# Layer 1 of a four-layer kernel: squared halves added before the length matmul, reciprocal lengths spread through DRAM, first image one chunk ahead

## The chip, the cores and the metric

The kernel runs on one core of a Trainium2 chip, in float32 throughout. The metric is the device time of one execution in microseconds (us). Beside the timed runs there is one execution recorded by the hardware profiler; all times inside the kernel come from that one.

## What is computed

The input is four images of 56 x 56 tokens with 256 channels. Four attention-like layers follow one another, each normalised in front and added to its input. The change lies in the second of them (layer 1), whose reference, per image with n = 3136 tokens, is

```python
xn = x / jnp.maximum(jnp.linalg.norm(x, axis=-1, keepdims=True), EPS)
A = jnp.einsum('bnc,cc,bmc->bnm', xn, W_adj, xn)
A = jnp.exp(5.0 * (A - jnp.max(A, axis=-1, keepdims=True)))
A = A * (1.0 - jnp.eye(n, dtype=A.dtype))
A = A / jnp.maximum(jnp.sum(jnp.abs(A), axis=-1, keepdims=True), EPS)
rowsum = jnp.sum(A, axis=-1, keepdims=True)
xW = jnp.einsum('bnc,dc->bnd', x, W_aff)
Ax = jnp.einsum('bnm,bmc->bnc', A, x)
AxW = jnp.einsum('bnc,dc->bnd', Ax, W_aff)
diff = rowsum * (xW + b_aff) - AxW
```

followed by a normalisation over the channels and a leaky ReLU. `x` is here the group-normalised input of the layer. What matters for the change is the first line: every token's vector is scaled to length 1, so each token needs the sum of its 256 squares, and its reciprocal square root has to reach every channel.

## The kernel before

**Layout.** Channels lie on the 128 partitions, in two halves (`CC` = 2); tokens run along the free axis. An image's 3136 tokens are 24 tiles of 128 and a rest of 64 (stored twice, to fill a 25th tile). `tokens` (L1339) prepares an image in seven chunks of up to four tiles: chunks 0 to 5 hold four tiles (512 tokens), chunk 6 (`NC4`) only the rest. Since the channels are on partitions, a sum of squares is a sum over partitions, which TensorE (PE) takes.

**One chunk's steps.** `load` fetches x from DRAM into `x0` (L1349, L1352). `normal(h)` normalises half h on VectorE (DVE, L939) into `xn`; after the second half ScalarE (ACT) squares both into `x0` (L1358). `lengths` sums the squares with matmuls of one column, two per tile (L1366), into PSUM; DVE clips them into `rn` (L1368, one number per token, tokens on partitions), GpSimd (POOL) takes the power -1/2 (L1369) and multiplies it into an identity matrix, `dg` (L1370). `values(i0)` multiplies two tiles by W_aff (L1379) and copies them to `xw` (L953 on DVE or L955 on ACT). `unit_length` multiplies a matrix of ones by `dg` (L1387), which puts every token's reciprocal length on all partitions in PSUM, and DVE multiplies `xn` by it into `xnT` (L1389). For chunk 6, POOL then scales `xdr` (L1393).

**The main work.** A unit is one row tile j and up to four column tiles. `scaled` (L1404, POOL) prepares the row tile `xd`, `logits` (L1411) multiplies it with `xnT`, ACT takes the exponential (L1414), POOL masks the diagonal (L1416), `transposed` transposes the result (L1502, copied at L1505), and `products` multiplies it with `xw` by columns (L1521, added into `acc` by DVE, L1443) and by rows (L1516). A, being symmetric before its rows are divided, is computed once for both. The rest tile has its own forms (`rest_logits` L1453, `rest_products` L1482 and L1486). When a row tile is done, `finish` normalises it on DVE and POOL (L1557 to L1580), and `add` transposes it back (L1587) and adds it to the residual (L1595), which is stored (L1599) while the next one is loaded (L1544).

**What sets the order.** In layer 1 the orders of PE and DVE are those in which the program writes the instructions; those of ACT, POOL and of the DMA queue on SyncE (SP) are set by a scheduler when the kernel is built. Each engine runs its instructions in order. The loop over units calls `small_step` twice per unit; it takes the first entry of the list `small` whose due time has come. The chunks of image b+1 are prepared beside the units of image b: `replace` (L1659), called at row tiles 3, 6, 10, 14, 16, 19 and 23 for chunks 6, 0, 1, 2, 3, 4 and 5, first runs whatever is still pending of earlier chunks (`now`, L1652), loads the chunk, and puts its steps into `small`, due twelve tiles later. `begin` (L1668) runs the pending steps of a chunk at once where a unit needs it. The first image has nothing beside which it could be prepared; a loop of its own (L1628 to L1632) goes through its chunks in order: normalise the next chunk, then `values`, `lengths`, `values` and `unit_length` of this one.

**Buffers.** In layer 1 the PSUM tag "m" has one bank, shared by `lengths`, `values`, `unit_length` and `add`; "v", which the column products use, has two. `x` and `xn` have two buffers each, `dg` one. In the first image the four tags "v", "o", "t" and "s" are used in turn.

Of the kernel before, what the change touches and what calls it, by code (L numbers as in the profile page):

```python
# [24 lines left out]
FP = mybir.dt.float32  # L25
I32 = mybir.dt.int32
AF = mybir.ActivationFunctionType
ALU = mybir.AluOpType
# [3 lines left out]
NIMG = 4  # L32
# [3 lines left out]
P = 128  # L36
CC = C // P
# [14 lines left out]
TINY = 1e-12  # L52
# [778 lines left out]
def direct_blocks(ctx: ExitStack, tc: tile.TileContext, d: dict, watch):  # L831
# [3 lines left out]
    nc = tc.nc  # L835
    const = ctx.enter_context(tc.tile_pool(name="dconst", bufs=1))
    dram = ctx.enter_context(tc.tile_pool(name="ddram", bufs=1, space=bass.MemoryType.DRAM))
    ps = None
    no_step = lambda: None
# [6 lines left out]
    def tokens_of(l, b, t0, n):  # L846
        return stream_of[l][b].rearrange("(h p) t -> p h t", p=P)[:, :, t0:t0 + n]
# [8 lines left out]
    ident = const.tile([P, P], FP, name="ident")  # L856
    make_identity(nc, ident)
    ones = const.tile([P, P], FP, name="ones")
    nc.vector.memset(ones, 1.0)
    mhalf = const.tile([P, CC], FP, name="mhalf")  # L860
# [9 lines left out]
    def psum_tile(tag, bufs, banks=1):  # L870
        shape = [P, 512] if banks == 1 else [P, banks, 512]
        return ps.tile(shape, FP, tag=tag, name="ps_" + tag, bufs=bufs)
# [60 lines left out]
    def known(l, b):  # L933
        while (l, b) not in stats:
            pending.pop(0)()
        return stats[l, b]

    def normalise(dst, src, gst, h):
        nc.vector.tensor_scalar(dst, src, gst[:, h, 0:1], gst[:, h, 1:2], ALU.subtract, ALU.mult)  # L939
# [10 lines left out]
    def evac(i, dst, src):  # L950

        if i % 2:
            nc.vector.tensor_copy(dst, src)  # L953
        else:
            nc.scalar.copy(dst, src)  # L955
# [366 lines left out]
    def layer1(early, big, pool, late, next_layer):  # L1322


        NB, REST = divmod(T, P)
        NC4 = NB // 4
# [5 lines left out]
        xnT = big.tile([P, CC, (NB + 1) * P], FP, name="xnT")  # L1332
        xw = big.tile([P, NB + 1, C + 1], FP, name="xw")
        xdr = big.tile([P, CC, P], FP, name="xdr")
        offd = big.tile([P, P], FP, name="offd")
        nc.vector.tensor_scalar(offd, ident, -1.0, 1.0, ALU.mult, ALU.add)
        nc.vector.memset(xw[:, :, C:], -1.0)

        def tokens(b, c, ps_a=ps_m):  # L1339

            tiles = range(4 * c, min(4 * c + 4, NB + 1))
            k, m = P, len(tiles)
            n = m * P
            box = {}

            def load():
                x = box["x0"] = early.tile([P, CC, 512], FP, tag="x", name="x1")
                if c < NC4:
                    nc.sync.dma_start(out=x[:, :, :n], in_=tokens_of(1, b, 4 * c * P, n))  # L1349
                else:  # L1350
                    for i in range(2):
                        nc.sync.dma_start(out=x[:, :, i * REST:(i + 1) * REST], in_=tokens_of(1, b, NB * P, REST))  # L1352
                box["x"] = early.tile([P, CC, 512], FP, tag="xn", name="xn1")

            def normal(h):
                normalise(box["x"][:, h, :n], box["x0"][:, h, :n], known(1, b), h)
                if h:
                    nc.scalar.activation(box["x0"][:, :, :n], box["x"][:, :, :n], AF.Square)  # L1358

            def lengths():  # L1360
                pm, sq = ps_a(), box["x0"]
                rn = early.tile([P, 4, 1], FP, tag="rn", name="rn")
                dg = box["dg"] = early.tile([P, 4, P], FP, tag="dg", name="dg", bufs=1)
                for i, t in enumerate(tiles):
                    for h in range(CC):
                        nc.tensor.matmul(pm[:k, i:i + 1], lhsT=sq[:, h, i * P:i * P + k], rhs=ones[:, 0:1],  # L1366
                                         start=(h == 0), stop=(h == CC - 1))
                nc.vector.tensor_scalar_max(rn[:k, :m, 0], pm[:k, :m], TINY * TINY)  # L1368
                nc.gpsimd.tensor_tensor(rn[:k, :m, 0], rn[:k, :m, 0], mhalf[:k, 0:1].to_broadcast([k, m]), ALU.pow)  # L1369
                nc.gpsimd.tensor_tensor(  # L1370
                    dg[:k, :m, :k], ident[:k, :k].rearrange("p (o q) -> p o q", o=1).to_broadcast([k, m, k]),
                    rn[:k, :m, :].to_broadcast([k, m, k]), ALU.mult)

            def values(i0):
                pm = ps_a()
                mm = min(2, m - i0)
                for i in range(i0, i0 + mm):
                    for h in range(CC):
                        nc.tensor.matmul(pm[:k, (i - i0) * C:(i - i0 + 1) * C], lhsT=box["x"][:, h, i * P:i * P + k],  # L1379
                                         rhs=w_aff[:, h, :], start=(h == 0), stop=(h == CC - 1))  # L1380
                evac(i0 // 2, xw[:k, 4 * c + i0:4 * c + i0 + mm, :C],
                     pm[:k, :mm * C].rearrange("p (a b) -> p a b", b=C))

            def unit_length():

                pm = ps_a()
                nc.tensor.matmul(pm[:, :n].rearrange("p (m k) -> p m k", k=k), lhsT=ones[:k, :], rhs=box["dg"][:k, :m, :k],  # L1387
                                 start=True, stop=True)
                nc.vector.tensor_tensor(xnT[:, :, 4 * c * P:4 * c * P + n], box["x"][:, :, :n],  # L1389
                                        pm[:, :n].rearrange("p (o k) -> p o k", o=1).to_broadcast([P, CC, n]), ALU.mult)  # L1390
                if c == NC4:
                    for h in range(CC):
                        nc.gpsimd.tensor_scalar_mul(xdr[:, h, :], xnT[:, h, NB * P:], adj[:, h:h + 1])  # L1393

            return [load], [lambda h=h: normal(h) for h in range(CC)], [lambda: values(0), lengths] + [lambda i=i: values(i) for i in range(2, m, 2)] + [unit_length]

        xd, out, xr = {}, {}, {}
        y_rest = late.tile([REST, C + 1], FP, name="yr", bufs=1)
# [214 lines left out]
        for b in range(NIMG):  # L1613
            if b == 0:
                units += [(b, None, q) for q in range(2)]
            for j in range(NB):
# [3 lines left out]
                if b + 1 < NIMG and 0 <= j - 20 < 2:  # L1620
                    units.append((b + 1, None, j - 20))
        turn = iter(range(6 * (NC4 + 1)))
        fresh = [tokens(0, c, lambda: psum_tile(*(("v", 2), ("o", 2), ("t", 1), ("s", 2))[next(turn) % 4])) for c in range(NC4 + 1)]
        for c in range(2):
            fresh[c][0].pop()()
        for step in fresh[0][1]:
            step()
        for c in range(NC4 + 1):  # L1628
            for step in (fresh[c + 1][1] if c < NC4 else []) + fresh[c][2]:
                step()  # L1630
            if c + 2 <= NC4:
                fresh[c + 2][0].pop()()  # L1632
        small, done = [], 0
# [34 lines left out]
        def begin(w):  # L1668
            if w[1] is None:
                for c in (NC4, 2 * w[2], 2 * w[2] + 1):  # L1670
                    now((w[0], c))
                return rest_logits(w[2])
            now((w[0], (w[3] - 1) // 4))
            return logits(*w)
# [3 lines left out]
        for k, w in enumerate(units):  # L1678
            b, j, first = w[:3]
# [11 lines left out]
            ahead = begin(units[k + 1]) if k + 1 < len(units) else None  # L1691
# [567 lines left out]
```

## Time and profile before

| | us |
|---|---|
| median of the three timed runs | 3945.29 |
| their lowest and highest | 3945.14, 3947.95 |
| the profiled execution's own time | 3952.89 |
| its span, first to last instruction | 3951.1 |
| busy: PE, its weight loads (PEld) | 3774.7, 2533.5 |
| busy: DVE, ACT, POOL | 2369.0, 1379.9, 1752.2 |
| layer 1's first image prepared, about | 795 to 848 |
| layer 1's units, about | 848 to 2760 |

In a line of the timeline the columns are the start, the duration, the engine, the source line, the operation, output and inputs, and the shapes; "x8" means that eight instructions follow one another and were merged, and the brackets hold the idle time in front and what ended it. A matmul in float32 is two records. The end of a matmul is modelled, so prices of PE are read from starts. PE, PEld, DVE, ACT and POOL are the engines; SPq is the queue of SP, which issues the DMAs. Clocks are given as a share of full speed.

### The profile page before, as it was taken

How to read it: one execution, taken by the hardware profiler on the slowest of the kernel's cores; microseconds unless marked ns; L12 is line 12 of the kernel's file. 1: busy time of each engine (PE TensorE's matmuls, PEld its weight loads, DVE VectorE, ACT ScalarE, POOL GpSimd, SP SyncE). 2: the span in 40 equal slices, each digit the busy share in tenths (PEclk: the TensorE clock that was granted, in tenths of full speed). 3: DMA queues.
4: the chain of work that ended last, by engine and by line, in shares of the span. 5: the costliest groups of instructions: out<-in, count | busy, mean ns of one | idle time of the engine just before them, and what ended most of it. 6: DMA issues, size and time to landing. Idle time of an engine off the chain costs nothing. (4 is left out here: it accounts for less than half of the span.)

```text
span 3951.1 us, 112757 instructions
## 1 busy us (share of the span) xinstructions
PE 3774.7 (96%) x49095; PEld 2533.5 (64%) x49095; DVE 2369.0 (60%) x4431; ACT 1379.9 (35%) x2927; POOL 1752.2 (44%) x1883
## 2 busy tenths in 40 slices
PE   6899999889999999999999999999999999899998
PEld 3455555557777677776777767776566666455554
DVE  6777777734345544445444553446788888577775
ACT  3354545422222222222222222222555555344443
POOL 2576767721123312233112331124677777555555
PEclk9899999989999999999999999999999999899998
DMA  7343333320000100001000000001344443434443
GB/s 266 101 140 118 120 116 113 101 105 1 25 19 25 40 3 18 15 30 35 6 18 22 21 29 1 20 10 43 112 133 122 136 120 119 152 123 131 138 132 94
DMA packets 268739, 303.13 MB, mean 77 GB/s; under 512 B 25927, under 2 KB 260585, under 8 KB 267753
## 3 DMA queue, kind: packets, MB, share of 16 engines
q1 hardware_dynamic: 267946, 295.76, 24.0%
q8 instruction: 387, 6.34, 0.6%
q14 instruction: 118, 0.96, 0.1%
q10 hardware_dynamic: 288, 0.08, 0.0%
HBM read 203.39 MB, written 92.37 MB: 75 GB/s over the span
## 5 line engine op out<-in xcount | busy, mean ns | idle before, releaser
L1443 DVE TENSOR_TENSOR acc<-acc,ps_v 128x257 f32<-128x257 f32 x1104 | 463.3, 423 | 718.9 <-PE ps_v L1521 690.8
L1521 PE MATMUL ps_v<-xw,e 128*128 128x257 f32 x2208 | 612.9, 382 | 1.2 <-DVE acc L1443 1.2
L1516 PE MATMUL ps_o<-xw,at 128*128 128x257 f32 x2208 | 609.2, 380 | 0.0
L1411 PE MATMUL ps_s<-xnT,xd 128*128 128x512 f32 (+3 forms) x1344 | 572.9, 549 | 3.9 <-DVE xnT L1389 3.9
L1505 ACT COPY at<-ps_t 128x512 f32<-128x512 f32 (+3 forms) x332 | 170.4, 513 | 970.1 <-PE ps_t L1502 969.8
L1080 POOL TENSOR_TENSOR b<-e 126x336 f32<-126x336 f32 (+5 forms) x512 | 502.1, 1001 | 13.4 <-ACT e L1068 5.2
L1521 PEld LDWEIGHTS ps_v<-xw,e 128*128 128x128 f32 x2208 | 414.4, 190 | 141.8 <-issue 82.2
L1516 PEld LDWEIGHTS ps_o<-xw,at 128*128 128x128 f32 x2208 | 419.9, 190 | 59.2
L946 PE MATMUL ps_m<-xn,w_wqkv 128*32 128x392 f32 x4096 | 380.8, 501 | 16.4 <-DVE vt L977 5.2
L1404 POOL TENSOR_SCALAR xd<-xnT,vec 128x128 f32<-128x128 f32 x192 | 116.8, 619 | 569.2 <-PE ps_s L1411 565.8
L1071 POOL TENSOR_TENSOR e<-e,m0t 126x672 f32<-126x672 f32 (+3 forms) x128 | 239.5, 1871 | 250.3 <-ACT e L1070 245.3
L1071 POOL TENSOR_TENSOR e<-e,bias 119x784 f32<-119x784 f32 (+5 forms) x128 | 244.2, 1908 | 168.2 <-ACT e L1070 167.5
L1411 PEld LDWEIGHTS ps_s<-xnT,xd 128*128 128x128 f32 x1344 | 226.3, 191 | 141.6 <-issue 126.3
L1414 ACT ACTIVATE e<-ps_s 128x512 f32<-128x512 f32 x336 | 185.3, 552 | 348.1 <-PE ps_s L1411 341.1
L992 ACT ACTIVATE no<-rs 128x168 f32<-128x168 f32 (+2 forms) x256 | 93.9, 367 | 561.6 <-DVE rs L1843 257.6
L1089 PEld LDWEIGHTS ps_o<-e,vp 124*32 124x32 f32 (+3 forms) x8192 | 205.2, 113 | 108.9 <-issue 88.3
L946 PEld LDWEIGHTS ps_m<-xn,w_wqkv 128*32 128x32 f32 x4096 | 124.2, 111 | 196.9 <-issue 130.7
L1089 PE MATMUL ps_o<-e,vp 124*32 124x112 f32 (+3 forms) x8192 | 239.8, 253 | 6.7 <-POOL e L1071 5.1
L1068 ACT ACTIVATE e<-e 126x672 f32<-126x672 f32 (+5 forms) x256 | 219.6, 858 | 26.2 <-DVE e L1067 13.4
L939 DVE TENSOR_SCALAR xn<-x,gst 128x28 f32<-128x28 f32 (+4 forms) x368 | 206.4, 611 | 31.1 <-PE ps_m L946 22.4
L1843 DVE RECIPROCAL rs<-ps_o 128x196 f32<-128x196 f32 (+2 forms) x128 | 175.6, 1372 | 78.1 <-PE ps_o L1089 74.5
L1021 POOL TENSOR_TENSOR e<-e,m3l 98x784 f32<-98x784 f32 x64 | 119.7, 1870 | 210.5 <-ACT e L1018 210.5
(196 smaller groups left out, 6161.0 us busy)
## 6 DMA issues: line engine op xcount, KB each, us to landing
x<-xr SPq DMA_DIRECT2D x64, 392.0 KB
x<-in_x SPq DMA_DIRECT2D x53, 448.0 KB
x<-x SPq DMA_DIRECT2D x60, 392.0 KB
xr<-x SPq DMA_DIRECT2D x60, 392.0 KB
vd<-v SPq DMA_DIRECT2D x72, 256.0 KB
xr<-in_x SPq DMA_DIRECT2D x32, 392.0 KB
xr<-x SPq DMA_DIRECT2D x28, 448.0 KB
x<-xr SPq DMA_DIRECT2D x28, 448.0 KB
```

The lines of the kernel that those rows point to most:

```text
L939: nc.vector.tensor_scalar(dst, src, gst[:, h, 0:1], gst[:, h, 1:2], ALU.subtract, ALU.mult)
L946: nc.tensor.matmul(pm[j * HD:(j + 1) * HD, :n], lhsT=w[:, h, col + j * HD:col + (j + 1) * HD], rhs=rhs(h), start=(h == 0), stop=(h == CC - 1))
L1068: nc.scalar.activation(ev, ev, AF.Exp)
L1071: nc.gpsimd.tensor_tensor(parts(ev), parts(ev), w["emask"], ALU.mult)
L1080: nc.gpsimd.tensor_tensor(w["b"][a][:nk, :, :2 * nq].rearrange("p h (i c) -> p h i c", i=2), ev[:, :, :, 0, :], ev[:, :, :, 1, :], ALU.add)
L1089: nc.tensor.matmul(w["o"](k, i)[j * HD:(j + 1) * HD], lhsT=ones[:nk, :HD] if k else v(j, u), rhs=w["b"][j // 2][:nk, j % 2, i * nq:(i + 1) ...
L1411: nc.tensor.matmul(s[:, :n], lhsT=xd[j][:, h, :], rhs=xnT[:, h, first * P:last * P], start=(h == 0), stop=(h == CC - 1))
L1414: nc.scalar.activation(e[:, :n], s[:, :n], AF.Exp, scale=5.0)
L1443: nc.vector.tensor_tensor(acc[:, i, :], acc[:, i, :], pv[:, :C + 1], ALU.add)
L1516: nc.tensor.matmul(out[j][:, :C + 1], lhsT=e[:, col(i)] if i == j else at[:, col(i)], rhs=xw[:, i, :], start=(i == j), stop=(i == NB - 1))
L1521: nc.tensor.matmul(pv[:, :C + 1], lhsT=e[:, col(i)], rhs=xw[:, j, :], start=True, stop=True)
L1843: nc.vector.reciprocal(rs.rearrange("p (t c) -> p t c", t=2), pv[:, :, 1, :])
```

## The change

It has three parts.

- After squaring, POOL adds the second half of the squares to the first, and `lengths` uses one matmul per tile on the sum, for all images.
- For images 1 to 3 and all chunks but chunk 5, `rn` is written by DMA from SP to a row of a new DRAM tensor `shares` (four numbers of 4 bytes per partition), and a second DMA reads the row back to all 128 partitions, into the buffer that `dg` had; the DVE multiply takes it from there (SBUF), without `dg` and without the matmul with ones. Chunk 5 and the first image keep `dg` and the matmul.
- The steps are reordered. In images 1 to 3 two empty steps come first, then `lengths`, the two `values`, for the chunks by DMA five empty steps, and `unit_length`. In the first image, `lengths` of a chunk runs before the `unit_length` of the chunk in front of it, and both `values` of a chunk come together.

```diff
@@ -1332,6 +1332,7 @@
         xnT = big.tile([P, CC, (NB + 1) * P], FP, name="xnT")
         xw = big.tile([P, NB + 1, C + 1], FP, name="xw")
         xdr = big.tile([P, CC, P], FP, name="xdr")
+        shares = dram.tile([NIMG, (NB + 1) * P], FP, name="shares")
         offd = big.tile([P, P], FP, name="offd")
         nc.vector.tensor_scalar(offd, ident, -1.0, 1.0, ALU.mult, ALU.add)
         nc.vector.memset(xw[:, :, C:], -1.0)
@@ -1341,6 +1342,7 @@
             tiles = range(4 * c, min(4 * c + 4, NB + 1))
             k, m = P, len(tiles)
             n = m * P
+            by_dma = b > 0 and c != NC4 - 1
             box = {}
 
             def load():
@@ -1355,21 +1357,26 @@
             def normal(h):
                 normalise(box["x"][:, h, :n], box["x0"][:, h, :n], known(1, b), h)
                 if h:
-                    nc.scalar.activation(box["x0"][:, :, :n], box["x"][:, :, :n], AF.Square)
+                    sq = box["x0"]
+                    nc.scalar.activation(sq[:, :, :n], box["x"][:, :, :n], AF.Square)
+                    nc.gpsimd.tensor_tensor(sq[:, 0, :n], sq[:, 0, :n], sq[:, 1, :n], ALU.add)
 
             def lengths():
                 pm, sq = ps_a(), box["x0"]
                 rn = early.tile([P, 4, 1], FP, tag="rn", name="rn")
-                dg = box["dg"] = early.tile([P, 4, P], FP, tag="dg", name="dg", bufs=1)
-                for i, t in enumerate(tiles):
-                    for h in range(CC):
-                        nc.tensor.matmul(pm[:k, i:i + 1], lhsT=sq[:, h, i * P:i * P + k], rhs=ones[:, 0:1],
-                                         start=(h == 0), stop=(h == CC - 1))
-                nc.vector.tensor_scalar_max(rn[:k, :m, 0], pm[:k, :m], TINY * TINY)
-                nc.gpsimd.tensor_tensor(rn[:k, :m, 0], rn[:k, :m, 0], mhalf[:k, 0:1].to_broadcast([k, m]), ALU.pow)
-                nc.gpsimd.tensor_tensor(
-                    dg[:k, :m, :k], ident[:k, :k].rearrange("p (o q) -> p o q", o=1).to_broadcast([k, m, k]),
-                    rn[:k, :m, :].to_broadcast([k, m, k]), ALU.mult)
+                for i in range(m):
+                    nc.tensor.matmul(pm[:, i:i + 1], lhsT=sq[:, 0, i * P:(i + 1) * P], rhs=ones[:, 0:1], start=True, stop=True)
+                nc.vector.tensor_scalar_max(rn[:, :m, 0], pm[:, :m], TINY * TINY)
+                nc.gpsimd.tensor_tensor(rn[:, :m, 0], rn[:, :m, 0], mhalf[:, 0:1].to_broadcast([P, m]), ALU.pow)
+                box["share"] = early.tile([P, 4, P], FP, tag="dg", name="dg", bufs=1)
+                if by_dma:
+                    row = shares[b:b + 1, 4 * c * P:4 * c * P + n]
+                    nc.sync.dma_start(out=row.rearrange("o (m p) -> p (o m)", p=P), in_=rn[:, :m, 0])
+                    nc.sync.dma_start(out=box["share"].rearrange("p m k -> p (m k)")[:, :n], in_=row.to_broadcast([P, n]))
+                else:
+                    nc.gpsimd.tensor_tensor(
+                        box["share"][:, :m, :], ident.rearrange("p (o q) -> p o q", o=1).to_broadcast([P, m, P]),
+                        rn[:, :m, :].to_broadcast([P, m, P]), ALU.mult)
 
             def values(i0):
                 pm = ps_a()
@@ -1383,16 +1390,23 @@
 
             def unit_length():
 
-                pm = ps_a()
-                nc.tensor.matmul(pm[:, :n].rearrange("p (m k) -> p m k", k=k), lhsT=ones[:k, :], rhs=box["dg"][:k, :m, :k],
-                                 start=True, stop=True)
+                share = box["share"].rearrange("p m k -> p (m k)")[:, :n]
+                if not by_dma:
+                    pm = ps_a()
+                    nc.tensor.matmul(pm[:, :n], lhsT=ones, rhs=share, start=True, stop=True)
+                    share = pm[:, :n]
                 nc.vector.tensor_tensor(xnT[:, :, 4 * c * P:4 * c * P + n], box["x"][:, :, :n],
-                                        pm[:, :n].rearrange("p (o k) -> p o k", o=1).to_broadcast([P, CC, n]), ALU.mult)
+                                        share.rearrange("p (o k) -> p o k", o=1).to_broadcast([P, CC, n]), ALU.mult)
                 if c == NC4:
                     for h in range(CC):
                         nc.gpsimd.tensor_scalar_mul(xdr[:, h, :], xnT[:, h, NB * P:], adj[:, h:h + 1])
 
-            return [load], [lambda h=h: normal(h) for h in range(CC)], [lambda: values(0), lengths] + [lambda i=i: values(i) for i in range(2, m, 2)] + [unit_length]
+            steps = [lambda i=i: values(i) for i in range(0, m, 2)]
+            if b:
+                steps = [no_step] * 2 + [lengths] + steps + [no_step] * (5 if by_dma else 0)
+            else:
+                steps += [lengths]
+            return [load], [lambda h=h: normal(h) for h in range(CC)], steps + [unit_length]
 
         xd, out, xr = {}, {}, {}
         y_rest = late.tile([REST, C + 1], FP, name="yr", bufs=1)
@@ -1623,11 +1637,14 @@
         fresh = [tokens(0, c, lambda: psum_tile(*(("v", 2), ("o", 2), ("t", 1), ("s", 2))[next(turn) % 4])) for c in range(NC4 + 1)]
         for c in range(2):
             fresh[c][0].pop()()
-        for step in fresh[0][1]:
+        for step in fresh[0][1] + fresh[0][2][-2:-1]:
             step()
         for c in range(NC4 + 1):
-            for step in (fresh[c + 1][1] if c < NC4 else []) + fresh[c][2]:
+            *make, _, scale = fresh[c][2]
+            ahead = fresh[c + 1] if c < NC4 else ([], [], [])
+            for step in ahead[1] + make + ahead[2][-2:-1]:
                 step()
+            scale()
             if c + 2 <= NC4:
                 fresh[c + 2][0].pop()()
         small, done = [], 0
```

## What I predict

> **What bounds the kernel now.** I read the table of busy time by stretch first, cut where layer 1 begins (780), where its first image's preparation ends (848.3), and at the image boundaries. The numbers after each stretch are its length and then the busy time of PE, its weight loads, DVE, ACT and POOL (records in brackets), the granted clock and the DMA share.
>
> ```profile
> 780.00:848.30 68.30, 53.28 (x311) 39.92 (x311) 27.43 (x49) 18.35 (x26) 23.56 (x28) 0.84 0.45 168
> 848.30:1368.00 519.70, 517.27 (x2331) 374.15 (x2332) 230.12 (x596) 115.63 (x217) 122.49 (x191) 0.99 0.06 20
> 1368.00:1853.00 485.00, 481.51 (x2176) 355.08 (x2174) 224.20 (x581) 105.07 (x196) 124.35 (x192) 1.00 0.07 21
> ```
>
> From 848 on PE is busy 99% at full clock, DVE under half, POOL a quarter, and the DMA engines are nearly idle. So PE time taken out there shortens the span one for one, unless its cover goes too. The 53 us from 795 to 848 are another stage: PE waits in turn for POOL and DVE there.
>
> **What leaves PE while it is full.** In the timeline of PE for chunk 1 of image 1, a program matmul is two records (f32), and a price is the distance from its start to the start of what follows:
>
> ```profile
> 1177.23 1.84 PE L1366 MATMUL ps_m<-ones,x 128*128 128x1 f32 x16
> 1178.93 1.11 PE L1521 MATMUL ps_v<-xw,e 128*128 128x257 f32 x4
> ...
> 1184.52 1.02 PE L1387 MATMUL ps_m<-dg,ones 128*128 128x512 f32 x2
> 1185.38 0.60 PE L1516 MATMUL ps_o<-xw,e 128*128 128x257 f32 x2
> ```
>
> Lengths (L1366): 8 matmuls in 1.70 us, 0.2125 each. The added halves need one per tile instead of two: 25 fewer per image, 75 in images 1 to 3: **-15.9 us**. Spreading (L1387): 0.86 us for a 512-wide one, 0.22 for the 128-wide one (998.67 to 998.89). By DMA go chunks 6 and 0 to 4 of images 1 to 3, chunk 5 stays a matmul: 15 x 0.86 + 3 x 0.22 = **-13.6 us**. Sum -29.5.
>
> **What the order makes of "seven steps ahead".** The change inserts empty steps, but `replace` and `begin` flush whatever is pending. In the changed instruction order, DVE runs between `rn` and the multiply 8 accumulator adds for chunk 6, 13 and 12 for chunks 0 and 1, but 1, 5 and 5 for chunks 2, 3 and 4: those are flushed by the next chunk's `replace`. For chunk 2 PE has, behind the lengths: one transpose 0.11, logits 1.72, values 1.72, a column and a row 0.87, values 1.72 = 6.14; then DVE copies `xw` (0.89 from there to its end), so DVE reaches the multiply 7.0 us after the lengths. By the same rows 8.5 for chunk 3, 10.5 for chunk 4, over 11 for the rest.
>
> The chain that must arrive by then: lengths to `rn` 0.34, POOL's power 0.08 + 1.04 (behind it on POOL: diagonal mask, `u`, `rstd`; the 1.04 us of `dg` that followed it is gone), then two DMA legs. Nearest rows, in SP's waits (us, times, longest):
>
> ```profile
> SPq L2049 <- DMA vd<-vt: 63.9, 28, 3.7
> SPq L1544 <- DMA x<-xr: 56.2, 25, 2.7
> ```
>
> Both are a store through DRAM that something on SP waits for: 2.28 and 2.25 mean behind the issue (0.36). Two legs 5.3, chain 6.7 us; at the longest wait, 8.1, chain 9.6. No row shows the 512 pieces of 4 bytes that `rn` is written in. The bounds: nothing more; or 512/16 x 57 ns (24.0% of 16 x 3951 us over q1's 267,946 packets) = 1.8, chain 11.4. I take 7 to 8, since the legs are single transfers on nearly idle engines. A chain of 7 to 8 makes DVE wait up to 1 us at chunk 2 only. Behind it are the residual add and the next unit's accumulator adds; PE needs their first bank back some 2.5 us later (transposes 0.33, logits 1.72, a row 0.43). So it costs nothing here.
>
> The Trainium skill ("DMA: Bandwidth & Descriptors", Specifications) speaks against this store: below 512 bytes a transfer does read-modify-write. No run here shows what that costs; if it doubled the first leg, the chain would be near 9.4 and the sum below unchanged.
>
> SP's queue: each pair of DMAs follows a load of `x` that waited for the same or an earlier `lengths`, so nothing is late in front of it; the residual store and load behind it start up to 6 us later, and have tens of us (1017 and 1020, 1103 and 1105). The new multiply reads `share` from SBUF where it read PSUM: 1.22 us before; the bounds are 0.6 (the two-input SBUF form L1580 has 0.42 per 256) and 1.7 (twice 0.86), and I take 1.2; DVE has half its time free.
>
> POOL: per chunk +1.28 for the add (interpolated between L1576, 727 ns for 256 elements, and L1021, 1870 for 784), -1.04 for `dg`, beside 360 idle us per image. The mask L1416 and `xd` are what PE could wait for; the add stands in front of them by several us. Zero, at worst 1 us per chunk (18).
>
> The skill ("GPSIMD Engine Reference", Specifications) says a DVE instruction with two SBUF inputs contends with GpSimd, which the new multiply becomes. The trace agrees: `dg` took 1.26 us beside L1580 and 1.04 without. For 18 multiplies that is a few us of POOL time with room to spare.
>
> **What the flush costs at chunk 5.** Before and after it ends a unit's supply of `xnT`:
>
> ```profile
> 1371.20 1.89 PE L1379 MATMUL ps_m<-w_waff,xn 128*128 128x256 f32 x8
> 1372.93 0.60 PE L1502 MATMUL ps_t<-ident,e 128*128 128x128 f32 x4
> 1373.97 1.10 PE L1387 MATMUL ps_m<-dg,ones 128*128 128x512 f32 x2 [0.44 <-DVE xw L953]
> 1376.38 1.99 PE L1411 MATMUL ps_s<-xnT,xd 128*128 128x512 f32 x4 [1.31 <-DVE xnT L1389]
> ```
>
> Now PE loses 0.61 (transposes end 1373.36) + 1.55 (2.41 less 0.86) = 2.16 us per image. In the changed order it is transposes, values, values, spread, logits in one go on the only `ps_m` bank: a bank handed from values to values (ACT, about 0.95), to spread (DVE, 1.04), then 1.55: 3.54. **+1.4 per image, +4.2.** At chunk 2 the transposes L1587 now wait for `xw` (1.04) instead of the multiply (0.62): **+1.2** for three. Both ends: 0 (if the neighbours cover them) and 9.
>
> **The first image (795 to 848).** A round lasts 7.06 us (L1387 at 821.17 and 828.23): DVE normalises, ACT squares, PE lengths, DVE, POOL power and mask, spread, multiply, each waiting for the one before. After: from the multiply's end, normalise 1.08, square 0.07 + 1.06, add 0.1 + 1.28, lengths 0.1 + 0.85, spread 0.86 + 0.2, multiply 1.22 = 6.8; power and `dg` move off it. Five rounds save 1.3. The last, small chunk loses its tail: -2.3 in its round (normalise, square, add of 128 columns fit beside the values) and -1.7 between its multiply and `rest_logits` (now 3.56). The start loses: PE begins with lengths that need square and add, at 798.4 instead of 795.3, and the granted clock is 0.50 until 806; +2.2. Net **-3.1**, bounds -7 and +1.
>
> **Sum.** -29.5 + 4.2 + 1.2 - 3.1 = -27.2 us. The profiled execution took 3952.89 (span 3951.1 and 1.8 around it) and would take 3925.7; the runs' median is 3945.29, 7.6 lower, and I keep the difference: **3918 us**.
>
> **Rivals.**
> 1. *Half of it.* The -29.5 is real PE work, but small waits take its place: mask or `xd` late on POOL (18), `ps_m` handovers at 9 instead of 5.4, the first image at +1. 29.5 - 9 - 1 - up to 9 (half of POOL's bound) leaves about 11 to 15: 3932. For it: `ps_m` has one bank and the new order puts its users closer. Against: PE's idle time per image is now only 3.5 us, so waits are rare.
> 2. *Slower: the DRAM round trip is late where the flush cuts it short.* DVE is in order; the multiply holds the accumulator adds, and with two `ps_v` banks PE stops. It decides from a chain of about 14 us: with 2.5 us of slack the stalls per image are 4.5 + 3 + 1 + 0.5 = 9, the whole gain over three images. At 16 us: 6.5 + 5 + 3 + 2.5 = 17, 51 in all, +24: 3969. Needed: a 4-byte store that takes over 9 us. For it: no row shows such a store. Against: the bound above is 11.4.
> 3. *It doesn't bring PE time.* If the lengths and spreads were hidden by waits, nothing would come: 3945. Against: in the fence above the next instruction starts at once after both.
>
> **Chances.** Forecast 0.63 (3908 to 3928), rival 1 0.18 (3928 to 3940; a few of these are within 0.2%), rival 2 0.14 with everything from 3953 up, rival 3 and chains near 14 us 0.05. A measurement of this kernel can tell about 0.2% (8 us) from no change. Faster 0.63 + 0.16 = 0.79, same 0.07, slower 0.14. The range 3908 to 3940 holds 0.81: forecast and rival 1; its lower end is no handover cost and the first image at -7.
>
> **What would show it.** L1366's successor with 200 records and the spread with 20 instead of 56; PE idle before the logits of chunk 5 near 3.5 us per image in three places; DVE's wait for the DMA of `share` below 2 us at chunk 2 and none elsewhere; rounds of 6.8 in the first image. Wrong, if DVE waits for `share` by 5 us or more, if POOL's mask releases PE late, or if the stretches of images 1 and 2 shrink by less than 6 us each.

## The result, and where the time went

| | median us | runs | span of the profiled execution | clock | layer 1, from its first normalisation to its last column matmul |
|---|---|---|---|---|---|
| before | 3946.33 | 4 (3945.14 to 3947.95) | 3951.1 | 0.977 | 1950.2 |
| after | 3993.89 | 4 (3992.38 to 3997.0) | 3990.5 | 0.973 | 1998.2 |

After is **slower**, by a ratio of 1.012 [1.0105, 1.0135]: 48 us where I had forecast 27 less. Layer 1 accounts for all of it (+48.0). The two spans differ by only 39, because the layers behind it, which the change doesn't touch, took 1206 us in the profiled execution of before and 1197 in that of after. So below I read layer 1 from its own marks and not from the span.

First the table of busy time by stretch, for after, cut where the three lines of before were cut. The last three numbers are the granted clock, the DMA share and GB/s.

```profile
780.00:848.30 68.30, 50.41 (x257) 36.07 (x258) 25.83 (x47) 18.30 (x27) 30.64 (x31) 0.78 0.45 162
848.30:1368.00 519.70, 497.08 (x2215) 358.76 (x2214) 226.76 (x587) 112.48 (x212) 125.45 (x194) 0.98 0.09 22
1368.00:1853.00 485.00, 464.59 (x2062) 340.39 (x2060) 215.03 (x558) 103.29 (x192) 121.88 (x186) 0.99 0.08 21
```

In the second and third stretch PE is now idle for 22.6 and 20.4 us, where it was idle for 2.4 and 3.5. An image, counted from the `rn` of its chunk 6 to that of the next image, takes 500.5 and 501.4 us (484.1 and 485.8 before). That is 16.4 and 15.6 more; with a third at that rate and +2.0 in the first image it makes 50, for 48 measured.

The same table for image 1 alone, between those two marks, first before and then after:

```profile
995.29:1479.40 484.11, 480.62 (x2171) 354.35 (x2171) 223.74 (x579) 105.06 (x197) 123.51 (x191) 1.00 0.07 22
```
```profile
996.25:1496.74 500.49, 476.14 (x2110) 348.94 (x2109) 224.05 (x580) 105.55 (x196) 125.97 (x192) 0.98 0.10 24
```

PE's busy time fell by only 4.5 us, because 6.0 of it in after are work drawn out by a lower clock (below). Its work at full clock fell from 480.6 to 470.2, which is 10.5 for 9.8 worked out; idle time rose from 3.5 to 24.35. Image 2 leaves the same work, 480.6 and 470.2.

What PE waits for comes from the table of waits, for after (us in all, times, longest), first of the computing engines, then of SP's queue:

```profile
DVE xnT L1398 <- DMA dg<-shares: 50.6, 11, 8.0
PE ps_v L1535 <- DVE acc L1457: 39.6, 15, 5.7
PE ps_m L1601 <- DVE xr L1609: 20.5, 6, 6.4
```
```profile
SPq L1375 <- DMA shares<-rn: 156.8, 18, 9.6
SPq L2066 <- DMA vd<-vt: 64.1, 28, 4.2
```

DVE's multiply waits up to 8 us for the spread lengths, and PE waits in turn for the accumulator adds and residual adds queued behind it. Before, PE's wait at the same `acc` was 1.2 us in all:

```profile
PE ps_v L1521 <- DVE acc L1443: 1.2, 3, 0.4
```

The second fence of after holds the reason: the load of `share` waits 8.7 us on average for the store of `rn`. The row below it, which I took as the nearest price, is still at 2.29 on average.

The same on one chunk: chunk 2 of image 1 in the timeline of after (start, duration, engine, line; in brackets the idle time before and its releaser):

```profile
1254.05 0.16 DVE L1369 TENSOR_SCALAR rn<-ps_m 128x4 f32<-128x4 f32 x1 [1.23 <-PE ps_m L1368]
1254.29 1.04 POOL L1370 TENSOR_TENSOR rn<-rn,mhalf 128x4 f32<-128x4 f32 x1 [3.25 <-DVE rn L1369]
1255.36 0.36 SPq L1374 DMA_DIRECT2D shares<-rn  x1
...
1260.45 0.68 DVE L953 COPY xw<-ps_m 128x512 f32<-128x512 f32 x1
...
1264.59 0.33 SPq L1375 DMA_DIRECT2D dg<-shares  x1
1269.12 1.22 DVE L1398 TENSOR_TENSOR xnT<-xn,dg 128x1024 f32<-128x1024 f32 x1 [7.99 <-DMA dg<-shares]
1271.07 0.80 PE L1535 MATMUL ps_v<-xw,e 128*128 128x257 f32 x1 [5.66 <-DVE acc L1457]
```

DVE is free for the multiply at 1261.13, 7.1 us after `rn`; the data is there 15.1 us after `rn`. The store leg takes 9.2 us, the load leg 4.5. The single DMA packets in the trace show that those of the 512 pieces have ended by 1257.6; the other 7 us pass until SP sees the store complete. Chunks 3 and 4 go the same way, 17.0 and 17.6 us from `rn` to the multiply; for each, the multiply and PE's stall behind it:

```profile
1308.19 1.23 DVE L1398 TENSOR_TENSOR xnT<-xn,dg 128x1024 f32<-128x1024 f32 x1 [4.33 <-DMA dg<-shares]
1310.13 1.23 PE L1535 MATMUL ps_v<-xw,e 128*128 128x257 f32 x2 [5.60 <-DVE acc L1457]
...
1353.47 1.23 DVE L1398 TENSOR_TENSOR xnT<-xn,dg 128x1024 f32<-128x1024 f32 x1 [4.13 <-DMA dg<-shares]
1355.08 0.69 PE L1601 MATMUL ps_m<-ident,y 128*128 128x128 f32 x2 [6.42 <-DVE xr L1609]
```

A stall costs more than its length. The stretches at the end of chunk 2's stall and behind it, in after:

```profile
1269.00:1271.00 2.00, 0.00 (x0) 0.00 (x0) 1.88 (x4) 0.00 (x0) 0.00 (x0) 0.89 0.00 0
1271.00:1273.00 2.00, 1.93 (x5) 1.56 (x6) 1.09 (x4) 0.00 (x0) 1.17 (x2) 0.50 0.03 8
1273.00:1275.00 2.00, 2.00 (x9) 1.42 (x8) 0.00 (x0) 0.42 (x1) 0.28 (x1) 0.76 0.00 0
1275.00:1277.00 2.00, 2.00 (x8) 1.22 (x7) 0.32 (x1) 0.77 (x2) 0.08 (x1) 1.00 0.00 0
```

PE comes back at half clock. The clock's own records give three such spells in image 1, one at each stall:

```profile
1270.57:1273.98 3.41, 2.91 (x7) 2.25 (x8) 1.52 (x5) 0.00 (x0) 1.45 (x2) 0.50 0.02 5
1308.11:1314.94 6.83, 4.81 (x11) 3.38 (x12) 4.33 (x10) 0.27 (x1) 1.45 (x2) 0.50 0.03 10
1352.49:1359.32 6.83, 4.24 (x12) 2.83 (x13) 4.86 (x12) 0.48 (x1) 0.72 (x1) 0.50 0.22 77
```

Each begins before PE is back, and idle time at half clock costs nothing more. PE works 12.0 us in them, so they cost 6.0 us. In before, image 1 has no such spell and image 2 has one of 3.41 us at 1860.95, behind the flush at chunk 5. It cost 1.7 us, which is why before's second image is longer than its first.

**Theories.** A: the DMA chain takes about 16 us and is late wherever a flush leaves it 7 to 13 us. Rival B: the new order of the steps costs it (lengths ahead of the values, empty steps, everything flushed in one go on the one `ps_m` bank). Rival C: the halves added on GpSimd, the DMAs or the multiply from SBUF slow their neighbours.

### The profile page after: what moved, and what is told of

Its sections match the earlier page's. It is cut to its first block, busy times and chain, and to the rows that moved or that the text cites. A ratio compares the mean times of both kernels' runs of the same rounds, so it can differ in the third digit from the quotient of the medians.

```text
span 3990.5 us, 112350 instructions
## 1 busy us (share of the span) xinstructions
PE 3747.4 (94%) x48859; PEld 2505.8 (63%) x48859; DVE 2369.5 (59%) x4431; ACT 1381.1 (35%) x2927; POOL 1767.2 (44%) x1893
## 4 chain that ended last, share of the span: by engine, by line
PE 80%; DVE 9%; DMA 4%; POOL 2%; issue 2%; ACT 1%; SPq 0%; DVEq 0%; POOLq 0%; ACTq 0%
PE ps_m L946 17%; PE ps_o L1530 13%; PE ps_s L1425 12%; PE ps_v L1535 12%; PE ps_m L973 6%; PE ps_o L1089 5%; PE ps_s L1060 4%; PE ps_t L1516 3%; PE ps_o L1029 2%; DMA shares<-rn 2%; PE ps_s L1014 1%; DVE e L1067 1%; DVE rs L1239 1%; DMA dg<-shares 1%; DVE xn L939 1%
## 5 line engine op out<-in xcount | busy, mean ns | idle before, releaser
L1080 POOL TENSOR_TENSOR b<-e 126x336 f32<-126x336 f32 (+5 forms) x512 | 502.6, 1002 | 12.7 <-ACT e L1068 4.6
L1070 ACT ACTIVATE e<-ps_s 126x672 f32<-126x672 f32 (+5 forms) x256 | 206.0, 805 | 20.1 <-PE ps_s L1060 20.1
```

The costliest lines, as they stand in the source:

```text
L1070: nc.scalar.activation(ev, sv, AF.Exp)
L1080: nc.gpsimd.tensor_tensor(w["b"][a][:nk, :, :2 * nq].rearrange("p h (i c) -> p h i c", i=2), ev[:, :, :, 0, :], ev[:, :, :, 1, :], ALU.add)
```

## The experiments

Medians are of each kernel's runs, ratios against the kernel before on the same chip. "An image" is the distance between two `rn` of chunk 6, as above.

### 1 to 4: each suspect alone

**e1_matmul**, A against B and C:

```diff
-            by_dma = b > 0 and c != NC4 - 1
+            by_dma = False
```

> The changed kernel with every chunk spread by the matmul again; the added halves, the new order of the steps and the new first image stay. If the late DMA chain is the cause, no DVE wait is left at the multiply, PE's idle time before the transposes of the residual add goes, and the lengths still save 15.9 us: 3951 - 15.9 + 5.4 (handovers at the flushes) + 2.3 (first image, as measured) = 3943 by the span, 3935 to 3945. If the new order, the add on GpSimd or the squares' longer way is the cause, it stays above 3970.

Measured: 3943.65, ratio 0.9992 [0.9982, 1.0002]; an image 487.0 and 485.3. So the DMA costs 50 us net, as A says. (That 3943 was forecast is partly luck: its base, the profiled 3951, lies some 5 us above the median.) But the 15.9 us of the lengths don't show either, and 5.4 for handovers had been too few. PE's idle time of 0.4 us or more in image 1 is 6.9 us, and the clock drops twice (3.41 us each, some 1.6 us lost each time). The first place is the flush at chunk 2, in the timeline of PE:

```profile
1256.82 1.10 PE L1396 MATMUL ps_m<-dg,ones 128*128 128x512 f32 x2 [0.99 <-POOL rstd L1586]
1259.23 0.69 PE L1601 MATMUL ps_m<-ident,y 128*128 128x128 f32 x2 [1.31 <-DVE xnT L1398]
```

With the lengths, values and spread handed to PE in one go, the spread waits for GpSimd and the transposes for the multiply. So B holds too, at 8.4 and 6.7 us an image against e5: 4.7 of idle time, 3.3 and 1.6 of clock.

**e2_more_room**, A by distance:

```diff
-                steps = [no_step] * 2 + [lengths] + steps + [no_step] * (5 if by_dma else 0)
+                steps = [lengths] + steps + [no_step] * (5 if by_dma else 0)
-                small[:0] = [(done + 12, step, (b, c)) for step in steps]
+                small[:0] = [(done + wait_for.get(c, 12), step, (b, c)) for step in steps]
-        begin_at = {3: NC4, 6: 0, 10: 1, 14: 2, 16: 3, 19: 4, 23: 5}
+        begin_at = {3: NC4, 5: 0, 8: 1, 12: 2, 15: 3, 19: 4, 23: 5}
+        wait_for = {3: 10, 4: 6}
```

> The changed kernel with the same DMAs, but chunks 0, 1, 2 and 3 of the next image begin one or two units' rows earlier (5, 8, 12, 15 instead of 6, 10, 14, 16), the two empty steps ahead of the lengths are gone, and chunks 3 and 4 are due sooner. In the order of DVE 13 to 15 accumulator adds then lie between the lengths and the multiply of chunks 0 to 4, where 1 to 5 lay for chunks 2 to 4. If the cost is the chain (about 16 us) being cut short, the waits at chunks 2, 3 and 4 go and the matmul time saved shows: about 3951 - 29.5 + 4 + 2.3 = 3928, 3920 to 3938. If the DMAs or the multiply from SBUF cost by themselves (contention, POOL slowed), it stays above 3965.

Measured: 3965.22, ratio 1.0047 [1.0029, 1.0064]; an image 492.7 and 491.8. Neither forecast: the DVE wait for `share` is gone altogether, but my own edit put another in its place. From the waits of this kernel:

```profile
PE ps_m L1368 <- POOL x L1362: 25.2, 15, 5.5
```

The two empty steps had given normalise, square and add their time; without them PE arrives at the lengths first (this wait falls to 5.9 us in e6, which has them). Inconclusive until e6.

**e3_16_bytes**, the price of the store:

```diff
-                    nc.sync.dma_start(out=row.rearrange("o (m p) -> p (o m)", p=P), in_=rn[:, :m, 0])
+                    nc.sync.dma_start(out=row.rearrange("o (p m) -> p (o m)", p=P), in_=rn[:, :m, 0])
...
+                if by_dma:
+                    for h in range(CC):
+                        nc.vector.tensor_tensor(xnT[:, h, 4 * c * P:4 * c * P + n].rearrange("p (m k) -> p m k", k=P),
+                                                box["x"][:, h, :n].rearrange("p (m k) -> p m k", k=P),
+                                                share.rearrange("p (k m) -> p m k", m=m), ALU.mult)
```

> The changed kernel with the reciprocal lengths stored so that a partition writes its four values side by side: 128 pieces of 16 bytes instead of 512 of 4, 2 KB in a row in DRAM; the order is untangled in the multiply, which becomes two instructions over strided reads. If the price goes with the number of pieces below 512 bytes, the time from the issue of the store to the issue of the load falls from about 9.5 us to 4 or less, and the kernel to about 3945. If a small store has a fixed time until its completion is seen, this stays at 8 to 10 us and the kernel at 3985 to 4000.

Measured: 3954.23, ratio 1.0018 [1.0008, 1.0027]; an image 487.3 and 488.3. The store of chunk 2, in this kernel's timeline:

```profile
1256.45 0.33 SPq L1374 DMA_DIRECT2D shares<-rn  x1
1259.34 0.33 SPq L1375 DMA_DIRECT2D dg<-shares  x1
```

2.9 us where it was 9.2; over the 15 such stores 1.4 to 3.4. Chunk 6, still 128 pieces of 4 bytes here, stays at 7.8 to 8.5. It isn't the number of pieces, then (128 in both cases), and not small stores as such. The kernel lands between the two forecasts: 13.4 us of PE's idle time are left in image 1, against 24.35 in after.

**e4_first_image**, the measuring ahead: the loop before layer 1's units as in the kernel before, and `steps.insert(1, lengths)` for the first image.

> The changed kernel with the first image's steps in the order of the kernel before (measured inside its own round, after the first values); the added halves stay there. If the first image matters as the traces say (rest logits at 850.6 against 848.3), this gives back 1 to 3 us: about 3991. If the measuring ahead does save time and something else delays the stage, it is 2 to 5 us slower than the changed kernel.

Measured: 3993.89, ratio 1.0122 [1.0105, 1.0139]. The whole doesn't tell 3 us, but the marks do: from the first normalisation to the rest logits 49.2 us, against 55.6 in after and 53.6 in before. With halves added, this stretch takes 47.6 to 49.2 in the six kernels that have the old order, and 52.2 to 55.6 in the seven with the measuring ahead. The measuring ahead loses time.

### 5 to 8: one part kept, and more room done properly

**e5_halves**: the kernel before, and only

```diff
+                    sq = box["x0"]
...
+                    nc.gpsimd.tensor_tensor(sq[:, 0, :n], sq[:, 0, :n], sq[:, 1, :n], ALU.add)
-                    for h in range(CC):
-                        nc.tensor.matmul(pm[:k, i:i + 1], lhsT=sq[:, h, i * P:i * P + k], rhs=ones[:, 0:1],
-                                         start=(h == 0), stop=(h == CC - 1))
+                    nc.tensor.matmul(pm[:k, i:i + 1], lhsT=sq[:, 0, i * P:i * P + k], rhs=ones[:, 0:1],
+                                     start=True, stop=True)
```

> The kernel before with one part of the change: the squared halves added on GpSimd and one length matmul per tile. Order of the steps, spreading by matmul and the first image's order are those of before. If what ate the saved 15.9 us in the first experiment (3943.65 instead of 3927) is the new order of the steps (an image took 487.0 and 485.3 us there, 484.1 and 485.8 before) and the measuring ahead (52.2 us against 49.2 in the fourth), then an image takes 479 here, the first one 49.2, and the kernel 3951 - 15.9 - 4.4 = 3931, 3925 to 3936. If the add itself costs the time (PE waiting for GpSimd), it is 3940 to 3947.

Measured: **3922.88**, ratio 0.9943 [0.9926, 0.9959]; an image 478.6 twice, the first one 48.0. In the table by stretch its row of 848 to 1368 is

```profile
848.30:1368.00 519.70, 515.52 (x2310) 371.85 (x2308) 233.91 (x604) 116.30 (x219) 131.98 (x200) 1.00 0.07 21
```

at full clock: 5.5 and 7.2 us an image gained for 5.3 worked out, where 1.7 of the 7.2 are the spell of lower clock in before's second image. The kernel is faster than forecast, whose base was again the profiled 3951. The add costs PE nothing, so that part of C falls.

**e6_room_kept_gap**: e2 with the two empty steps back and `wait_for = {0: 10, 1: 10, 2: 10, 3: 8, 4: 1}`.

> The second experiment again with its new wait taken out: the chunks begin as early as there, but the two empty steps ahead of the lengths stay, and the steps are due sooner instead (1 to 10 tiles after the start, not 12). In the order 8 accumulator adds lie between lengths and multiply for chunk 6, 13 or 14 for chunks 0 to 4; the stores stay 4 bytes wide. If the late chain was all that was wrong, no wait for the spread lengths and none for the add on GpSimd is left, and an image takes 484.1 - 9.8 + 1 to 3 = 476 to 478: 3925 to 3935. If DMA traffic, the two-input multiply or GpSimd contention cost by themselves, it is above 3945.

Measured: 3943.01, ratio 0.9992 [0.9983, 1.0002]; an image 484.1 twice, though 9.8 us of PE's work are out. A's wait is down to 3.9 us in all, all of it at chunk 6; the time lies between the two forecasts. What is left stands in PE's timeline of this kernel:

```profile
1330.02 0.41 PE L1601 MATMUL ps_m<-ident,y 128*128 128x128 f32 x2 [1.09 <-DVE xr L1609]
...
1332.85 0.44 PE L1601 MATMUL ps_m<-ident,y 128*128 128x128 f32 x2 [0.70 <-DVE xr L1609]
...
1336.16 0.44 PE L1601 MATMUL ps_m<-ident,y 128*128 128x128 f32 x2 [1.92 <-DVE xr L1609]
```

Four residual adds follow one another on the one bank. An empty step is not free: it takes a turn of `small_step`, and the residual adds behind it in the list wait until `settle` calls them all at once.

**e7_combined**: e6 with e3's store and multiply, and chunk 5 and the first image in the order of before (`steps[:1] + [lengths] + steps[1:]` where `by_dma` is false).

> What the runs point to, together: halves added; the lengths spread by DMA with 16 byte pieces and the room of the sixth experiment; chunk 5, which is spread by matmul, and the first image in the order of the kernel before. If the explanation is complete: 3951 - 4.4 (first image) - 29.5 + 0 to 5 = 3917 to 3925, below the halves alone. If the strided multiply (2.2 to 2.7 us of VectorE instead of 1.22) or handovers take it back, it is 3930 to 3940, no better than the halves alone.

Measured: 3945.25, ratio 0.9991 [0.9981, 1.0001]; an image 485.1 and 486.6. Above both forecasts. The second one's reason is in the trace, but not alone: PE's wait for the residual adds is 15.3 us in all (12.7 in e6), and 8.6 for the accumulator adds (3.8 in e6), behind two strided multiplies of 1.10 us (mean) each in place of one of 1.22.

**e8_512_bytes**: after, with

```diff
+            def flip():
+                pt = ps_a()
+                nc.tensor.transpose(pt[:m, :P], box["rn"][:, :m, 0], ident)
+                rt = early.tile([4, P], FP, tag="rt", name="rt")
+                nc.vector.tensor_copy(rt[:m], pt[:m, :P])
+                row = shares[b:b + 1, 4 * c * P:4 * c * P + n]
+                nc.sync.dma_start(out=row.rearrange("o (m p) -> (o m) p", p=P), in_=rt[:m])
```

> The changed kernel, but TensorE transposes the reciprocal lengths and they are stored as four pieces of 512 bytes (one transpose, one copy, behind the first values); load and multiply as in the changed kernel, and no more room. If the width of a piece decides, the load is issued 1.5 to 3.5 us behind the store as with 16 bytes, and the kernel takes 3940 to 3955. If only the scattering of 512 pieces over DRAM mattered, it is the same. If any small store is seen late and the 16 bytes were an exception, the gap is 8 to 10 us and the kernel takes 3985.

Measured: 3944.06, ratio 0.9993 [0.9984, 1.0003]; an image 483.9 and 483.6 (500.5 in after), with no more room than in after. From its timeline:

```profile
1258.86 0.27 SPq L1385 DMA_DIRECT2D shares<-rt  x1
...
1260.08 0.33 SPq L1386 DMA_DIRECT2D dg<-shares  x1
1263.44 1.23 DVE L1405 TENSOR_TENSOR xnT<-xn,dg 128x1024 f32<-128x1024 f32 x1 [1.84 <-DMA dg<-shares]
```

1.2 us from store to load. With the late store gone, after loses 50 us of its time: A, from the other side. The DMAs and the multiply from SBUF are still there, so the rest of C, which e1 couldn't tell from A, falls too.

### 9 to 12: what the DMA can bring, and the store measured

**e9_three_by_dma**: e5's halves and orders, and `by_dma = b > 0 and c in (NC4, 0, 1)` with five empty steps behind the values.

> The halves alone (fifth experiment) with DMA spreading, 4 byte pieces, only for chunks 6, 0 and 1 of images 1 to 3, the three that nothing flushes: order of the steps as in the kernel before, five empty steps ahead of the multiply. 9 and 13 accumulator adds lie between. If PE work that leaves is gained where the chain has room: 3922.9 - 3 x (2 x 0.86 + 0.22) = 3917. If the matmul's 0.86 us only covered VectorE's multiply of 1.22 us (the changed kernel shows PE waits of 0.72 and 1.10 us behind the multiplies of chunks 0 and 1, none in the kernel before), the waits take it back: 3922 to 3924, no difference from the halves alone.

Measured: 3918.02, ratio 0.9936 [0.9922, 0.9949]; an image 477.4 and 477.2, 1.2 and 1.3 less than the halves alone where 1.94 of matmul go. The median lies on the first forecast; since its interval overlaps that of e5, the size rests on the image's distance alone.

**e10_slots_shared**: e6, chunk 5 and first image in the order of before, chunk 3 due one tile later, and in `small_step`

```diff
+                    if step is no_step:
+                        other = next((a for a in small if a[0] <= done and a[2] in (None, -1)), None)
+                        if other:
+                            small.remove(other)
+                        step = other[1] if other else step_stats
```

> The sixth experiment (4 byte pieces, early start, six chunks by DMA) with three edits: an empty step gives its turn to a residual add or a step of the next layer that is due; chunk 5 and the first image run in the order of before; chunk 3 is due one tile later. There the residual adds had come in a row (1 to 7 PE instructions apart, on one bank; at least 16 before) and PE waited 1.09, 0.70 and 1.92 us for it, then 3.4 us of lower clock per image. If that and the chunk 5 flush are the rest of the loss, an image takes 478.6 - 4.5 + 0 to 2 = 474 to 476, and the kernel 3908 to 3918. If something else is left, it is at 3925 to 3943.

Measured: **3910.18**, ratio 0.9908 [0.9893, 0.9923], as expected: an image 476.0 and 474.3, the first one 47.6. Its interval lies just below that of the halves alone (0.9926 to 0.9959, each against the kernel before on its own chip). It has every part of the change but the measuring ahead and chunk 5's new order, and its stores are still 4 bytes wide. The waits of this kernel show the chain covered, at 2.6 us in all:

```profile
DVE xnT L1398 <- DMA dg<-shares: 2.6, 3, 1.3
```

though the store is as slow as ever (in SP's waits):

```profile
SPq L1375 <- DMA shares<-rn: 149.2, 18, 9.7
```

**e11_piece_width**: widths side by side in after, with the store split by chunk, and e3's multiply for all of them but chunk 3:

```diff
+                    if c == 3 or m == 1:
+                        nc.sync.dma_start(out=row.rearrange("o (m p) -> p (o m)", p=P), in_=rn[:, :m, 0])
+                    elif c in (1, 2):
+                        w = early.tile([P, 4, 2], FP, tag="rw", name="rw")
+                        wide = w[:, :, 0:1] if c == 1 else w[:, 0:4:2, :]
...
+                        nc.sync.dma_start(out=row.rearrange("o (p a b) -> p (o a) b", p=P, b=c), in_=wide)
+                    else:
+                        nc.sync.dma_start(out=row.rearrange("o (p m) -> p (o m)", p=P), in_=rn[:, :m, 0])
```

> A measurement of the store alone, in the changed kernel's places: chunks 0 and 4 store 128 pieces of 16 bytes, chunk 2 the same bytes to the same addresses as 256 pieces of 8 (from a tile with gaps, filled by one more copy on GpSimd), chunk 1 as 512 pieces of 4, chunk 3 as 512 pieces of 4 in the changed kernel's order (128 bytes apart in the partitions' order), chunk 6 128 pieces of 4. Read is only the time from the store's issue to the load's. If it's the width of a piece: 16 bytes 1.5 to 3, chunk 1 like chunk 3 at 8 to 10, 8 bytes between or like one of them. If it's the order of the addresses, chunk 1 is like chunk 0.

From SP's timeline, chunks 0, 1, 2 and 3 of image 1, each a store and the load that waits for it:

```profile
1083.23 0.33 SPq L1382 DMA_DIRECT2D shares<-rn  x1
1085.83 0.33 SPq L1383 DMA_DIRECT2D dg<-shares  x1
1180.36 0.61 SPq L1380 DMA_DIRECT2D shares<-rw  x1
1187.61 0.34 SPq L1383 DMA_DIRECT2D dg<-shares  x1
1258.24 0.55 SPq L1380 DMA_DIRECT2D shares<-rw  x1
1262.59 0.34 SPq L1383 DMA_DIRECT2D dg<-shares  x1
1291.84 0.36 SPq L1375 DMA_DIRECT2D shares<-rn  x1
1301.06 0.33 SPq L1383 DMA_DIRECT2D dg<-shares  x1
```

Issue to issue, over the three images: 16 bytes 1.4 to 3.2 us, 8 bytes 4.3 to 4.5, 4 bytes in the order of the 16-byte stores' addresses 7.2 to 7.3, 4 bytes in the changed kernel's order 8.8 to 9.4. The width decides; the order of the addresses adds up to 2 us.

**e12_no_slots**: e10 without its edit in `small_step`.

> The tenth experiment with one edit undone: an empty step again uses up a turn. 13 or 14 accumulator adds still lie between lengths and multiply, chunk 5 and the first image keep the order of before. If it was the bunched residual adds that stood between the sixth (484.1 us an image) and the tenth (476.0 and 474.3), an image takes 480 to 484 and the kernel 3927 to 3942. If it was the order at chunk 5, an image takes 474 to 477 and the kernel 3910 to 3917.

Measured: 3928.94, ratio 0.9966 [0.9952, 0.998]; an image 479.5 and 481.1, at the lower edge of the first forecast. Sharing the turns is worth 3.5 and 6.8 us an image, with PE's wait for the residual adds again 12.7 us in all (1.5 in e10). The other part of the way from e6 is chunk 5, the first image and chunk 3's due time. Against e7, which differs only in the store's layout with its strided multiply and in chunk 3's due time, an image is 5.6 and 5.5 us shorter. So the 16-byte pieces seem to cost more on VectorE than they gave where the chain had room; no run separates them from the due time.

## Why the prediction was wrong, step by step

- **The chain's price: the step that failed.** The prediction took "7 to 8, since the legs are single transfers on nearly idle engines", bounded by 11.4. It priced the store from rows of wide stores (pieces of 1024 and 1792 bytes) and bounded the 4-byte pieces by the time of their packets. The packets had indeed ended 1.3 to 2.7 us after the issue. What I left out is the time until the store counts as complete, which no packet count holds: 9.2 us for the leg at chunk 2, against 2.6 to 4.4. The load leg took 4.5 instead of 2.6. Together 15 to 18 us from `rn` at chunks 2 to 4. I named a store "that takes over 9 us" as what rival 2 needs, and set aside the fact that no row showed such a store as if the bound had covered it.
- **The distances** were right at chunk 2, 7.1 us (7.0 worked out), and too short at chunks 3 and 4, 12.7 and 13.5 (8.5 and 10.5); no wait stands in the timeline at chunks 0 and 1, and up to 1.2 us at chunk 6. PE's slack of 2.5 us was right at chunk 2, where 7.99 of DVE's wait became 5.66 of PE's. At chunks 3 and 4 there was none: 4.33 and 4.13 became 5.60 and 6.42.
- **Rival 2**, priced +24 at 16 us, had the mechanism. Its 17 us of stalls an image against 17.7 measured in chunks 2 to 4 of image 1 are partly luck, since distances longer than worked out and the missing slack offset each other. It lacked the clock, 6.0 us in image 1, and the smaller waits that bring the added idle time to 20.9. From e5's 478.6, less 4.9 of spreading, plus 20.9 of idle time and 6.0 of clock, image 1 comes to 500.6, for 500.5 measured.
- **Lengths, -15.9**: right. In e5 PE's work at full clock is 475.1 us an image, 5.5 less than before, for 5.3.
- **Spreading, -13.6**: right as PE work (475.1 to 470.2 an image, 4.9 for 4.5), and partly kept where the chain is covered: e10's image is 2.6 and 4.3 us below e5's for 4.5. Chunks 0 and 1 suggest what the matmul had also done: it kept PE busy during DVE's multiply. Without it PE waited 0.72 and 1.10 us there in after.
- **Flush at chunk 5, +1.4 an image**: the idle time there rose from 1.75 to 2.87, so +1.1, and chunk 2's adds waited 0.45 us longer. But with the clock drops the order costs 8.4 and 6.7 us an image instead of 1.8: e1's 487.0 and 485.3 against e5's 478.6. The turns that empty steps take weren't in my sum at all. In after itself the adds keep nearly the order of before; in e6 and e12 they are bunched.
- **First image, -3.1**: not gained. It was +2.0 in after's profile and in e8's, but -1.1 to -1.4 in e1, e2, e3, e6 and e11, which have the same first image; so even its sign differs between executions. In after a round of it stands at half clock (the spread matmul takes 2.05 us at 817.54, 1.10 at 826.89), since PE waits longer there: 4.0 us for the add at 816.17. I had priced it at full clock. The halves in the old order save 4.4 to 6.
- **POOL and the multiply**: right. The add takes 1.28 us, the multiply 1.22, and GpSimd delays no lengths in after's images 1 to 3.
- **SP's queue**: right; no residual transfer is late in after.

The Trainium skill's read-modify-write below 512 bytes ("DMA: Bandwidth & Descriptors", Specifications) pointed the right way, and I weighed it with a doubling of one leg. For the time until such a store is seen complete, which is not the rate that the page speaks of, the runs put the large step elsewhere: 16-byte pieces, also below 512, cost 1.4 to 3.8 us against 1.1 to 2.2 for 512 bytes, and 4-byte pieces 7.2 to 10.3. What makes narrow pieces complete late isn't shown here.

## What to carry over

Price a transfer that something waits for by a row with its own width of piece, and if there is none, let that ignorance reach into the range and the chances instead of bounding it by packet time; from the store's issue to the multiply, chunk 2 took 13.8 us with 4-byte pieces and 4.6 with pieces of 512 bytes. Where work is moved from a busy engine to a slow path, count what every flush leaves between the two ends, and count an empty step as a turn taken from whatever shares the list. A PE stall of a few us cost its length and, in image 1 of after, 1.5 to 2.4 us of clock behind it; even two short waits in a row at a handover can take back what a stage has saved.

## Not expected of the hardware

- The time from issue to seen completion of a store to DRAM, by width of piece: 4 bytes 7.2 to 10.3 us (128 pieces 7.4 to 8.8, 512 pieces 7.2 to 10.3), 8 bytes 4.3 to 4.5, 16 bytes 1.4 to 3.8, 512 bytes 1.1 to 2.2. The packets of the 4-byte pieces themselves had ended 1.3 to 2.7 us after the issue.
- The granted clock falls after less than I had thought. The Trainium skill ("TensorE: Matmul & The Clock Gate", HAM oscillation) names idle gaps of more than about 3.4 us. The stalls of 5.6 to 6.4 us here agree, with spells of 3.41 or 6.83 us at 0.50. But in e10 a drop followed a single gap of 1.43 us at 1293.3, with narrow length matmuls behind it:

```profile
1294.00:1296.00 2.00, 1.25 (x11) 1.20 (x11) 1.86 (x6) 0.00 (x0) 2.00 (x4) 1.00 0.29 111
1296.00:1298.00 2.00, 2.00 (x8) 0.65 (x8) 0.24 (x2) 0.48 (x1) 2.00 (x4) 0.51 0.31 70
1298.00:1300.00 2.00, 2.00 (x8) 0.47 (x5) 0.00 (x0) 0.17 (x1) 0.48 (x1) 0.63 0.84 226
```

  and e8 had 12.0 us of idle time in image 1, the longest gap 2.14, without one drop. The kernel before shows both sides: the same gaps of 0.44 and 1.31 us at chunk 5 were followed by a drop in image 2 and by none in image 1. What decides between them stays open.
